# Step 1 of a top-p attention layer: exponentials ahead of the list, a shorter list after tested bounds, two extra tiles in place of three, GpSimd in written order

## The chip, the core and the metric

One NeuronCore of a Trainium2 chip runs the whole program. The metric is the device time of one execution in microseconds; the figure quoted is the median of several executions. VectorE (DVE), ScalarE (ACT), GpSimd (POOL), TensorE (PE; its weight loads are the row PEld) and the SyncE queue (SP) each take their instructions in order.

## The reference

A graph layer makes `x` (3327 rows of 256). A second layer, which is what matters here, then runs two steps of top-p attention and neighbourhood averaging:

```python
q = X @ W1.T @ W2.T;  k = X @ W3.T
probs = softmax(q @ k.T)
sp = probs sorted downwards;  cs = cumsum(sp)
keep = cs - sp < 0.9                    # the fewest columns that hold 0.9 of the row
A = probs * mask(keep);  A = A / max(A.sum(-1), 1e-12)
...
for n in range(2):
    A = top_p_attention(Xa)
    Xf = R @ Xf;  Xa = A @ Xa           # R: sparse adjacency plus identity, rows scaled
    Z = Z + Xf @ U1[n].T + Xa @ U2[n].T
out = layernorm(x + layernorm(x + Z))
```

## The kernel before

The 3327 rows are 26 tiles of 128 rows (the last has 127). Layer 0 and step 0 of layer 1 are untouched by the change. In step 1, item `i` runs from `NT` = 26 to 51, one per tile. The kernel never sorts a whole row. For each tile:

- `some_logits` multiplies q by k into PSUM and ScalarE copies 8 chunks of 416 columns into an array `l` (L1693, L1696).
- `eights` (L1709) takes the eight largest of each group of 167 columns: 20 MAX8, 160 candidates.
- `list_1` and `list_2` sort the first 72 of them, nine rounds of MAX8 and MATCH_REPLACE8 (L1727, L1729). `exp` (L1777) computes the exponentials of the row in two halves with their sums, `exp_list` (L1790) those of the list.
- `list_3` and `settle` make running sums of the list (L1797), find the smallest kept value `t`, the number `d` of ties to drop, and a flag for rows that the list can't settle.
- `mask` drops surplus ties by a MATCH_REPLACE8 over the row (`drop`, L1825) and multiplies by "at least t" (L1811). The result is the tile's attention.
- `product` turns the attention in 7 groups of four 128 x 128 blocks (`turn`: PE transposes, ACT copies) and multiplies it by `xu` (`times`, L1907). Between the groups it runs what `run` has put into seven *slots*. This is the order of the tile loop, for TensorE, ScalarE and VectorE, written out by hand; GpSimd's order in step 1 is the scheduler's.
- `propagate` does the sparse product from 5 gathered blocks (`gather`, L645, issued by GpSimd; `fetch` issues all five at once), `scaled` and `tile_end` add up, normalise twice and store. Mean and variance come from VectorE's batch-norm instructions (`moments`, L1869, L1871).
- `put_aside_1` and `put_aside_2` number the flagged rows and store what is known of each (`pay`: row, maximum, threshold, bound) by an indirect DMA into the table `left_over` (L1981).

Flagged rows are then done as extra ("hard") tiles of 128 rows, `HARD` = 3 of them. `close` at item `NT + CLOSE` (21) ends the first: later rows go to the others. Of an extra tile k, `hard_load` reads the table and gathers the rows, `hard_q` and `hard_exp` make its exponentials, `coarse_bound` tries three bounds on ScalarE with Relu and Sign sums, `bound` tries the rest on VectorE (L1831, one pass over the row each), `hard` takes the values below the bound (L2103), their eights, a list of 72, three `drop`s and the mask (L2132), and `hard_end` multiplies, normalises and stores. `ends` runs the three after the tile loop. If any row stays unsettled or there are too many, a slow version of everything runs after a test at the end.

Of the kernel before, what the change touches and what calls it, by code (L numbers as in the profile page):

```python
# [16 lines left out]
P = 128  # L17
# [73 lines left out]
GROUP = (208, 167)  # L91
LIST = (40, 72)
# [3 lines left out]
HARD = 3  # L96
PAY = 4

COARSE = 3
CUTS = tuple(2.0 ** -f for f in (4.0, 2.0, 1.0, 0.5, 0.25, 0.125))  # L100

CLOSE = 21
# [1069 lines left out]
class Layer1:  # L1172
# [474 lines left out]
    def first_1(self):  # L1647


        while self.phase <= EVERY0 * (NT - 1) + max(AT_0[k] for k in ("sign0", "sign1", "y_out")):  # L1650
            yield
        v = self.item(NT)
        self.item(NT + 1)
        self.fetch(NT)
        v.cand = self.candidates(v.r, GROUP[1], v.tag)
        ready, waiting = [], list(range(-(-N // GROUP[1])))
        for pair in self.chunks():
            while self.done * P < min(NT * P, HALF + pair[0][1] + LC):
                yield
            for i in (NT, NT + 1):  # L1660
                self.some_logits(i, pair)
                yield
            ready += [c for h, s in pair for c in range(h * HALF + s, min(N, h * HALF + s + LC))]
            have = set(ready)
            for g in list(waiting):
                if have.issuperset(range(g * GROUP[1], min(N, (g + 1) * GROUP[1]))):
                    waiting.remove(g)
                    self.eights(v.cand, v.l, v.r, GROUP[1], g * GROUP[1], min(N, (g + 1) * GROUP[1]))
            yield
# [52 lines left out]
    def sort(self, cand, r, length, tag):  # L1722

        nc = self.nc
        lst = self.work.tile([P, length], F32, tag="lst", name=f"lst{tag}")
        for k in range(0, length, 8):
            nc.vector.max(lst[:r, k : k + 8], cand[:r])  # L1727
            if k + 8 < length:
                nc.vector.match_replace(cand[:r], lst[:r, k : k + 8], cand[:r], -BIG)  # L1729
            yield lst  # L1730

    def settle(self, lst, before, last, thr2, r, drop, flag, tag):
# [5 lines left out]
        out = self.work.tile([P, length], F32, tag="outl", name=f"out{tag}")  # L1738
        nc.vector.tensor_scalar(out[:r], before, thr2[:r], None, ALU.is_ge)
        kept = self.work.tile([P, length], F32, tag="kept", name=f"kept{tag}")  # L1740
# [8 lines left out]
        nc.gpsimd.tensor_scalar(lim[:r], last[:r], lst[:r, length - 1 : length], None, ALU.max)  # L1749
        short = self.small("short", f"short{tag}")  # L1750
        nc.gpsimd.tensor_scalar(short[:r], lim[:r], t[:r], None, ALU.is_ge)
        many = self.small("many", f"many{tag}")
        nc.gpsimd.tensor_scalar(many[:r], d[:r], drop + 0.5, None, ALU.is_gt)
        nc.gpsimd.tensor_scalar(flag, many[:r], short[:r], None, ALU.max)
        return t, d, lim

    def list_1(self, i):

        nc, v = self.nc, self.items[i]
        n, r, tag = v.n, v.r, v.tag  # L1760
        if i > NT:
            v.cand = self.candidates(r, GROUP[n], tag)
            self.eights(v.cand, v.l, r, GROUP[n])
        v.last = self.last_eights(v.cand, r, tag)
        v.sort = self.sort(v.cand, r, LIST[n], tag)
        v.lst = next(v.sort)
        v.pay = self.st.tile([P, PAY], F32, tag="pay", name=f"pay{tag}", bufs=3)
        v.nmax, v.thr2 = v.pay[:, 1:2], v.pay[:, 2:3]
        nc.vector.tensor_scalar(v.nmax[:r], v.lst[:r, 0:1], -1.0, None, ALU.mult)
        v.p = self.p[i % 2]  # L1770
        v.sums = self.small("sums", f"sums{tag}", 2)
# [9 lines left out]
    def list_2(self, i):  # L1781
        for _ in self.items[i].sort:
            pass

    def exp_list(self, i):
        nc, v = self.nc, self.items[i]
        r, length = v.r, LIST[v.n]
        v.e = self.work.tile([P, length], F32, tag="e", name=f"e{v.tag}")
        nc.vector.memset(v.e[:, 0:1], 0.0)
        nc.scalar.activation(v.e[:r, 1:], v.lst[:r, : length - 1], AF.Exp, bias=v.nmax[:r])  # L1790

    def list_3(self, i):
# [3 lines left out]
        before = self.work.tile([P, LIST[n]], F32, tag="before", name=f"before{tag}")  # L1796
        nc.vector.tensor_tensor_scan(before[:r], v.e[:r], v.e[:r], 0.0, ALU.add, ALU.add)  # L1797
        nc.vector.tensor_scalar(v.thr2[:r], v.sums[:r, 0:1], v.sums[:r, 1:2], 2.0 * TOP_P, ALU.add, ALU.mult)
# [4 lines left out]
    def mask(self, i):  # L1803
# [5 lines left out]
        self.drop(v.l[:r], v.d, v.t, r, 0, tag)  # L1809
        sA = self.small("sA", f"sA{tag}")  # L1810
        nc.vector.scalar_tensor_tensor(  # L1811
            v.p[:r], v.l[:r, :N], v.t[:r], v.p[:r], ALU.is_ge, ALU.mult, accum_out=sA[:r]
# [21 lines left out]
    def fetch(self, i):  # L1834
# [6 lines left out]
        sh.gather(v.g, table, v.at)  # L1841
        v.m = self.work.tile([P, EB, P], F32, tag="m", name=f"m{v.tag}")
        nc.sync.dma_start(v.m, self.members[v.at])

    def propagate(self, i):
# [6 lines left out]
        nc.tensor.matmul(acc[:r, :D], self.ident[:r, :r], v.y, start=False, stop=True)  # L1852
        v.h1 = self.work.tile([P, D], F32, tag="xf2", name=f"h1_{v.tag}")[:r]
# [11 lines left out]
    def moments(self, src, r, tag):  # L1865
# [8 lines left out]
        return mv  # L1874

# [35 lines left out]
    def scaled(self, i):  # L1911
        nc, v = self.nc, self.items[i]
        v.h = self.work.tile([P, D], F32, tag="xa2", name=f"h{v.tag}")[: v.r]
# [18 lines left out]

    def tile_end(self, i):
# [4 lines left out]
        xb = self.work.tile([P, D], F32, tag="xt", name=f"xb{v.tag}", bufs=3)[:r]  # L1938
        move_rows(nc.sync, xb, sh.xb_rows[on, :], r)
        yield from self.output_rows(h, [xb], r, f"t{v.tag}")  # L1940
# [3 lines left out]
    def put_aside_1(self, i):  # L1944
# [4 lines left out]
        nc.gpsimd.tensor_copy(flag16, flag)  # L1949
        v.pos = self.psm.tile([P, 512], F32, tag="sm", name=f"pos{t}")  # L1950
# [35 lines left out]
    def hard_load(self, k):  # L1986
# [8 lines left out]
        tag_x, width = ("g", EB) if k == 2 else ("hx", 3)  # L1995
        v.x = self.work.tile([P, width, D], F32, tag=tag_x, name=f"x{tag}")
# [11 lines left out]
    def hard_q(self, k):  # L2008
# [14 lines left out]
        v.p = (*self.more, self.p[0])[k]  # L2023
        v.other = (self.l[0][:, :N], self.l[1][:, :N], self.p[1])[k]

        v.top = self.small(f"top{k}", f"top{v.tag}")
        nc.scalar.activation(v.top, v.pay[:, 3:4], AF.Exp, bias=v.pay[:, 1:2])
        nc.gpsimd.tensor_scalar(v.top, v.top, 1.0001, None, ALU.mult)
# [14 lines left out]
    def coarse_bound(self, k, cuts, junk):  # L2043
# [3 lines left out]
        tag = v.tag  # L2047
        less = self.small(f"less{k}", f"less{tag}")
        nc.gpsimd.tensor_scalar(less, v.pay[:, 2:3], 0.5 * (1.0 - 1e-5), None, ALU.mult)
        for f in cuts:  # L2050
            tag = f"{v.tag}_{f}"
            minus = self.small(f"minus{k}", f"minus{tag}")
            nc.gpsimd.tensor_scalar(minus, v.top, -f, None, ALU.mult)
            s = self.small(f"sums{k}", f"sums4{tag}", 4)
            for h in range(2):
                on = slice(h * HALF, min(N, (h + 1) * HALF))
                for j, func in enumerate((AF.Relu, AF.Sign)):
                    nc.scalar.activation(
                        junk[:, on], v.p[:, on], func, bias=minus, accum_out=s[:, 2 * h + j : 2 * h + j + 1]
                    )  # L2060
                    if h == 0 or j == 0:
                        yield
# [13 lines left out]
            yield  # L2076
            yield
            yield

    def bound(self, k, cuts):  # L2080
# [4 lines left out]
        nc.gpsimd.tensor_scalar(v.thr, v.pay[:, 2:3], 0.5, None, ALU.mult)  # L2085
# [11 lines left out]
    def hard(self, k):  # L2097
# [4 lines left out]
        sb = self.small("sb", f"sb{tag}")  # L2102
        nc.vector.scalar_tensor_tensor(other, v.p, top, v.p, ALU.is_lt, ALU.mult, accum_out=sb)  # L2103
        yield
        length = LIST[1]
        cand = self.candidates(P, GROUP[1], tag)
# [3 lines left out]
        for j, lst in enumerate(self.sort(cand, P, length, tag)):  # L2110
            if j == length // 16:
                yield
        e = self.work.tile([P, length], F32, tag="e", name=f"e{tag}")
        nc.vector.scalar_tensor_tensor(e[:, 0:1], thr, 1.0 / TOP_P, sb, ALU.mult, ALU.subtract)
        nc.vector.tensor_copy(e[:, 1:], lst[:, : length - 1])
        before = self.work.tile([P, length], F32, tag="before", name=f"before{tag}")
        nc.vector.tensor_tensor_scan(before, e, e, 0.0, ALU.add, ALU.add)
        flag = self.small("hf", f"hf{tag}")
        t, d, _ = self.settle(lst, before, last, thr2, P, HARD_DROP, flag, tag)

        late = self.small("late", f"late{tag}")
        nc.gpsimd.tensor_scalar(late, before[:, 0:1], thr2, None, ALU.is_ge)
        nc.gpsimd.tensor_scalar(flag, flag, late, None, ALU.max)
        real = self.small("real", f"real{tag}")
        nc.gpsimd.tensor_scalar(real, v.pay[:, 0:1], N - 0.5, None, ALU.is_lt)
        nc.gpsimd.tensor_tensor(self.hflag[:, k : k + 1], real, flag, ALU.mult)
# [11 lines left out]
    def hard_end(self, k):  # L2138
# [13 lines left out]
        v.end = self.output_rows(v.h, [self.b, x1], P, v.tag)  # L2152
# [34 lines left out]
    def ends(self, bounds, older, last):  # L2187


        open_ends, queue = [older, last], []  # L2190

        def more():
            if queue and next(queue[0], True):
                queue.pop(0)
            for g in open_ends[::-1]:
                if next(g, True):
                    open_ends.remove(g)

            for _ in range(2):
                for g in bounds:  # L2200
                    if not next(g, True):
                        break

        def start(k):
            yield from self.hard_q(k)
            for pair in self.chunks():
                yield
                self.hard_exp(k, pair)
            bounds.append(self.coarse_bound(k, CUTS[:COARSE], self.items[f"h{k}"].other))

        def end(k):
            yield from self.hard_end(k)
            open_ends.append(self.items[f"h{k}"].end)

        queue.append(start(2))
        for k in range(HARD):
            if k:
                for _ in bounds[k - 1]:
                    pass
                for _ in self.bound(k, CUTS[COARSE:]):  # L2220
                    more()
            for _ in self.hard(k):
                more()
            queue.append(end(k))
        self.whole()
        while queue or open_ends:
            more()
        for k in range(HARD):
            self.hard_store(k)
# [169 lines left out]
```

## Time and profile before

| | us |
|---|---|
| median of 3 runs (1795.28 to 1797.88) | 1795.72 |
| the profiled execution, its own time | 1795.22 |
| its span, first to last instruction | 1793.4 |
| first product of step 1 begins | 992.2 |
| last product of the tile loop begins | 1588.3 |
| VectorE done with extra tile 0, 1, 2 | 1657.9, 1711.9, 1760.3 |

| engine | busy us | share |
|---|---|---|
| PE | 1483.3 | 83% |
| DVE | 1414.3 | 79% |
| POOL | 1083.7 | 60% |
| ACT | 1023.2 | 57% |

How to read the views: a group or timeline row gives line, engine, operation, output tile <- input tiles, shapes and count; in groups then busy us, mean ns of one, and the idle time before it with what ended it. A row of the waits gives who waited at which line for whom: us in total, times, longest. A row of busy time by stretch gives from:to, its length, then busy us (and instructions) of PE, PEld, DVE, ACT, POOL, the granted PE clock, the DMA share and GB/s. "Idle" of an engine off the path costs nothing.

### The profile page before, as it was taken

The numbers are of one execution on the slowest core, as the hardware profiler recorded it, in microseconds if no ns is written. First come the engines' busy times: TensorE is split into PE (matmuls) and PEld (weight loads), VectorE is DVE, ScalarE is ACT, GpSimd is POOL, SyncE is SP. The second block draws the span as 40 slices with busy tenths as digits, with TensorE's granted clock in tenths as the row PEclk, the third lists the DMA queues.
The fourth block names the chain that finished last, engine by engine and source line by source line (L and its number), as shares of the span: only waits on it lengthen the run. The fifth ranks groups of instructions, "written<-read, shape, count | busy, mean of one in ns | idle before, by whom it ended". The sixth has DMA issues, their size and how long they took to land.

```text
span 1793.4 us, 27513 instructions
## 1 busy us (share of the span) xinstructions
PE 1483.3 (83%) x7995; PEld 998.1 (56%) x7995; DVE 1414.3 (79%) x4757; ACT 1023.2 (57%) x2286; POOL 1083.7 (60%) x1754
## 2 busy tenths in 40 slices
PE   6499999986999999999975999999999989872333
PEld 5256555553555555555543776666766666661333
DVE  5688888438878878878733999999999998787893
ACT  2366666646677777767742555555555555465511
POOL 1477777714666666656643567777777767474311
PEclk8789999987899999999998999999999999895666
DMA  8877774323344434433431222222222212100000
GB/s 237 290 272 236 238 237 123 86 68 96 102 115 122 109 106 116 123 103 105 123 79 51 57 65 69 68 68 68 66 65 66 64 51 77 37 16 21 4 3 3
DMA packets 102440, 179.58 MB, mean 100 GB/s; under 512 B 26401, under 2 KB 64799, under 8 KB 102282
## 3 DMA queue, kind: packets, MB, share of 16 engines
q0 software_dynamic: 26480, 74.24, 16.4%
q1 hardware_dynamic: 57548, 86.65, 14.7%
q10 hardware_dynamic: 18254, 16.86, 3.0%
q8 instruction: 65, 1.06, 0.2%
q14 instruction: 93, 0.76, 0.1%
HBM read 140.58 MB, written 37.21 MB: 99 GB/s over the span
## 4 chain that ended last, share of the span: by engine, by line
DVE 33%; PE 27%; POOL 17%; issue 11%; ACT 6%; DMA 5%; ACTq 1%; POOLq 0%; DVEq 0%
POOL g L645 8%; DVE cand L1709 6%; DVE array L1825 5%; DVE cand L1729 4%; DVE lst L1727 4%; DMA g<-x1k,uidx 3%; PE pl L1693 2%; DVE p L1811 2%; DVE array L1811 2%; POOL g L1525 2%; PE pav L1586 2%; PE pc L1349 2%; PE pavh L1907 2%; PE pav L1907 2%; PE pxf L1329 1%
## 5 line engine op out<-in xcount | busy, mean ns | idle before, releaser
L1907 PE MATMUL pav<-xu,at 128*128 128x256 f32 (+2 forms) x1352 | 331.4, 390 | 6.3 <-ACT at L1893 6.3
L1907 PEld LDWEIGHTS pav<-xu,at 128*128 128x128 f32 (+2 forms) x1352 | 246.1, 191 | 85.9 <-ACT at L1893 39.3
L1709 DVE MAX8 cand<-array 128x8 f32<-128x167 f32 (+5 forms) x921 | 241.5, 336 | 19.2 <-ACT array L1696 18.9
L1696 ACT COPY array<-pl 128x416 f32<-128x416 f32 (+3 forms) x402 | 183.1, 509 | 109.2 <-PE pl L1693 106.8
L1693 PE MATMUL pl<-kT,qT 64*128 64x416 f32 (+3 forms) x804 | 202.6, 566 | 8.4 <-ACT array L1696 4.5
L1893 ACT COPY at<-pt 128x512 f32<-128x512 f32 (+2 forms) x182 | 95.9, 542 | 143.2 <-PE pt L1891 143.0
L645 POOL DMA_INDIRECT g<-whx,edge x130 | 140.3, 1079 | 46.0 <-issue 36.2
L645 POOL DMA_INDIRECT g<-y_rows,edge x130 | 136.1, 1047 | 45.6 <-issue 29.8
L645 POOL DMA_INDIRECT g<-x_rows,edge x130 | 133.4, 1026 | 44.0 <-issue 33.5
L1525 POOL DMA_INDIRECT g<-x1k,uidx x130 | 136.6, 1051 | 32.2 <-issue 29.3
L1727 DVE MAX8 lst<-cand 128x8 f32<-128x160 f32 (+3 forms) x364 | 113.6, 312 | 8.1
L864 DVE FIND_INDEX8 at<-ones,array 128x8 uint32<-128x840 f32 (+1 forms) x104 | 105.5, 1027 | 0.0
L1693 PEld LDWEIGHTS pl<-kT,qT 64*128 64x128 f32 (+1 forms) x804 | 65.7, 187 | 69.0 <-issue 48.7
L1625 POOL TENSOR_TENSOR x<-x,c 128x256 f32<-128x256 f32 (+1 forms) x26 | 28.5, 1095 | 110.2 <-ACT c L1620 110.2
L1825 DVE MATCH_REPLACE8 array<-gone,array 128x3335 f32<-128x3335 f32 (+1 forms) x26 | 94.0, 3617 | 0.0
L1729 DVE MATCH_REPLACE8 cand<-lst,cand 128x160 f32<-128x160 f32 (+3 forms) x312 | 92.9, 298 | 0.0
L1926 POOL TENSOR_TENSOR h<-h,xb 128x256 f32<-128x256 f32 (+1 forms) x26 | 84.1, 3236 | 2.0
L1851 PE MATMUL pxf<-g,m 128*128 128x256 f32 (+1 forms) x260 | 67.5, 410 | 4.0 <-DVE base L1973 4.0
L985 PE MATMUL acc<-g,m 128*128 128x259 f32 (+1 forms) x260 | 65.0, 398 | 6.8 <-ACT m L981 6.8
L1851 PEld LDWEIGHTS pxf<-g,m 128*128 128x128 f32 (+1 forms) x260 | 50.1, 201 | 35.5 <-issue 24.0
L1586 PE MATMUL pav<-g,w 128*128 128x257 f32 (+1 forms) x260 | 62.6, 388 | 3.4 <-DVE w L1580 3.4
L1593 DVE TENSOR_SCALAR rA<-pav 128x1 f32<-128x1 f32 (+1 forms) x26 | 4.1, 158 | 77.1 <-PE pav L1586 77.1
(535 smaller groups left out, 3749.8 us busy)
## 6 DMA issues: line engine op xcount, KB each, us to landing
array<-in_adj_dram SPq DMA_DIRECT2D x23, 1248.0 KB
array<-in_adj_dram SPq DMA_DIRECT2D x23, 415.5 KB
members<-m SPq DMA_DIRECT2D x26, 320.0 KB
m<-members SPq DMA_DIRECT2D x26, 320.0 KB
whx<-table ACTq DMA_DIRECT2D x25, 129.5 KB
x_rows<-x ACTq DMA_DIRECT2D x25, 128.0 KB
x1k<-x ACTq DMA_DIRECT2D x25, 128.0 KB
xb_rows<-xb SPq DMA_DIRECT2D x25, 128.0 KB
```

Of the source, the lines that this page charges most:

```text
L645: self.nc.gpsimd.indirect_dma_start(out=dst[:, b, :], out_offset=None, in_=table[:, :], in_offset=bass.IndirectOffsetOnAxis(ap=self.edge[: ...
L864: nc.vector.max_index(at[:r, g, :], self.ones8[:r], ad[:r, g, :])
L1525: nc.gpsimd.indirect_dma_start(out=v.g2[:, b, :], out_offset=None, in_=sh.x1k[:, :], in_offset=bass.IndirectOffsetOnAxis(ap=v.idx[:, b : b ...
L1586: nc.tensor.matmul(v.acc[:r, : D + 1], v.w[:, b, :r], v.g2[:, b, : D + 1], start=(b == 0), stop=(b == UB - 1))
L1693: nc.tensor.matmul(pl[:r, :w], q[on], self.sh.kT[on, n, s : s + w], start=True, stop=True)
L1696: nc.scalar.copy(l[:r, h * HALF + s : h * HALF + s + w], pl[:r, :w])
L1709: self.nc.vector.max(cand[:r, g * 8 : g * 8 + 8], src[:r, g * group : min(N, (g + 1) * group)])
L1727: nc.vector.max(lst[:r, k : k + 8], cand[:r])
L1729: nc.vector.match_replace(cand[:r], lst[:r, k : k + 8], cand[:r], -BIG)
L1825: nc.vector.match_replace(rev, gone[:r], rev, -BIG)
L1851: nc.tensor.matmul(acc[:r, :D], v.m[:, b, :r], v.g[:, b, :], start=(b == 0), stop=False)
L1907: nc.tensor.matmul(v.acc[: v.r, :D], at[:k, j - 4 * g, : v.r], V[:k, j, :], start=(j == 0), stop=(j == NT - 1))
```

## The change

In each tile of step 1 the exponentials now come first. The groups have 104 columns (32 groups, 256 candidates). `highest` takes the row's maximum from the groups' first ranks, `exp_candidates` the exponentials of the candidates, and `list_1`, now on exponentials, tests four bounds (the maxima over groups of ranks 2 to 5): what the candidates at or above each add up to. Candidates above the best bound that is still short of the threshold are taken as one sum, and only 32 of the rest are sorted. `mask` works on the exponentials in place. Logits are computed three items ahead in place of two. Mean and variance of a tile come from two ScalarE passes with accumulators (`sums`, `by_sums`); extra tile 1 keeps the batch-norm form.

There are two extra tiles. The first closes behind tile 15, is loaded at tile 16, gets its exponentials at tile 17 and three coarse bounds on ScalarE in slots of tiles 18 to 24; its bounds and list on VectorE (`hard_first`) stand beside the last product. The second has two coarse and four fine bounds. GpSimd's order in step 1 is now written order too, and the gathers of the next tile are issued one by one in slots 2 to 6. In `hard`, settling's small operations move from GpSimd to VectorE.

```diff
-GROUP = (208, 167)
-LIST = (40, 72)
+GROUP = (208, 104)
+LIST = (40, 32)
+HARD_LIST = 72
+TRIED = (2, 6)
-HARD = 3
+HARD = 2
-COARSE = 3
+COARSE = (3, 2)
-CLOSE = 21
+CLOSE = 15
...
+    def highest(self, i):
...
+        nc.vector.tensor_reduce(v.nmax[:r], self.ranks(v.cand, r)[:, :, 0], AX.X, ALU.max, negate=True)
...
+    def list_1(self, i):
+        by_rank = ec[:r].rearrange("p (g e) -> p e g", e=8)
...
+        nc.vector.tensor_scalar(v.thr2[:r], v.sums[:r, 0:1], v.sums[:r, 1:2], 2.0 * TOP_P, ALU.add, ALU.mult)
+        nc.vector.tensor_reduce(high[:r], by_rank[:, first:end, :], AX.X, ALU.max)
+        v.last = self.last_eights(ec, r, tag)
+        for j in range(tried):
+            nc.vector.scalar_tensor_tensor(
+                v.cand[:r], ec[:r], high[:r, j : j + 1], ec[:r], ALU.is_ge, ALU.mult, accum_out=above[:r, j : j + 1]
+            )
+        nc.vector.tensor_scalar(over[:r], above[:r], 2.0, v.thr2[:r], ALU.mult, ALU.is_ge)
+        nc.vector.scalar_tensor_tensor(high[:r], over[:r], 2.0, high[:r], ALU.mult, ALU.max)
+        nc.vector.tensor_reduce(skip[:r], high[:r], AX.X, ALU.min)
+        nc.vector.scalar_tensor_tensor(v.cand[:r], ec[:r], skip[:r], ec[:r], ALU.is_lt, ALU.mult)
+        nc.vector.scalar_tensor_tensor(above[:r], over[:r], 0.5, above[:r], ALU.is_lt, ALU.mult)
+        nc.vector.tensor_reduce(v.e[:r, 0:1], above[:r], AX.X, ALU.max)
+        for _ in self.sort(v.cand, r, LIST[1], tag, v.lst):
+            pass
...
     def mask(self, i):
-        self.drop(v.l[:r], v.d, v.t, r, 0, tag)
+        self.drop(v.p[:r], v.d, v.t, r, 0, tag)
-            v.p[:r], v.l[:r, :N], v.t[:r], v.p[:r], ALU.is_ge, ALU.mult, accum_out=sA[:r]
+            v.p[:r], v.p[:r], v.t[:r], v.p[:r], ALU.is_ge, ALU.mult, accum_out=sA[:r]
...
+    def sums(self, h, r, tag):
+        nc.scalar.activation(junk[:r], h, AF.Identity, accum_out=s[:r])
+        nc.gpsimd.tensor_scalar(minus[:r], s[:r], -1.0 / D, None, ALU.mult)
+        yield
+        nc.scalar.activation(junk[:r], h, AF.Square, bias=minus[:r], accum_out=sq[:r])
+        nc.gpsimd.tensor_scalar(mv[:r, 1:2], sq[:r], 1.0 / D, LN_EPS, ALU.mult, ALU.add)
+        nc.gpsimd.tensor_tensor(mv[:r, 1:2], mv[:r, 1:2], self.power[:r], ALU.pow)
+        nc.gpsimd.tensor_tensor(mv[:r, 0:1], minus[:r], mv[:r, 1:2], ALU.mult)
+        yield
+        nc.scalar.activation(h, h, AF.Identity, bias=mv[:r, 0:1], scale=mv[:r, 1:2])
...
     def run(self):
-        with self.tc.manual_schedule(engines=engines):
+        with self.tc.manual_schedule(engines=engines | {mybir.EngineType.Pool}):
...
+                beside = self.propagate(i)
+                slot(1, next, beside)
+                slot(2, next, beside, None)
+                if i + 3 < total:
+                    for k, pair in enumerate(self.chunks()):
+                        slot((0, 1, 2, 6)[k], self.some_logits, i + 3, pair)
                 if i + 1 < total:
                     self.list_1(i + 1)
+                    slot(0, self.list_2, i + 1)
+                if i + 2 < total:
+                    for pair in self.chunks():
+                        slot(1, self.largest, i + 2, pair)
+                    slot(1, self.highest, i + 2)
+                    slot(3, self.exp_candidates, i + 2)
+                    slot(3, self.exp, i + 2, 0)
+                    slot(4, self.exp, i + 2, 1)
...
+                    slot(0 if late else 3, self.put_aside_2, i)
+                    slot(3, self.mask, i + 1)
...
+                for g in (1, 2, 5):
                     slot(g, next, older, None)
                     slot(g, next, last, None)
...
+                    for b, g in enumerate((2, 3, 4, 5, 6)):
+                        slot(g, self.neighbour, i + 1, b)
+                if closing == 1:
                     slot(0, self.hard_load, 0)
...
+                    first = self.hard_first()
+                    for g in range(7):
+                        slot(g, next, first, None)
                     slot(0, self.hard_load, 1)
...
     def ends(self, first, older, last):
+        for pair in self.chunks():
+            self.hard_exp(1, pair)
+            more()
+        for _ in self.coarse_bound(1, CUTS[: COARSE[1]], self.items["h1"].other):
+            more()
+        for _ in first:
+            pass
+        for _ in self.hard_end(0):
+            more()
...
+        for _ in self.bound(1, CUTS[COARSE[1] :]):
+            more()
+        for _ in self.hard(1):
+            more()
+        self.whole()
...
+        for _ in self.hard_end(1):
+            pass
```

## The prediction

> **What bounds the kernel now.** The page gives one profiled execution: 1795.22 us in all, span 1793.4, against a median of 1795.72; I sum against the span and add 1.8 at the end. The edit touches step 1 alone, so I asked first for busy time by stretch.
>
> ```profile
> core 0: us, PE busy (x) PEld busy (x) DVE busy (x) ACT busy (x) POOL busy (x), PEclk, DMA share, GB/s
> 1268.74:1291.86 23.12, 21.62 (x110) 16.13 (x109) 22.10 (x69) 12.72 (x25) 16.80 (x27) 1.00 0.24 66
> 1605.00:1660.00 55.00, 13.49 (x41) 7.03 (x40) 42.51 (x89) 27.58 (x41) 29.25 (x58) 0.54 0.08 22
> 1660.00:1711.00 51.00, 15.53 (x70) 12.77 (x69) 43.36 (x87) 21.89 (x30) 16.35 (x41) 0.67 0.01 3
> 1711.00:1761.00 50.00, 16.06 (x79) 13.85 (x79) 47.52 (x102) 5.63 (x11) 8.19 (x18) 0.67 0.01 3
> ```
>
> The first row is one ordinary tile: 23.12 us, VectorE 22.10 of it, TensorE 21.62. The other rows are the extra tiles: VectorE fills them and TensorE is a third busy. The chain of waits says the same: up to 1476 it is VectorE's mask (L1825, L1811) and eights (L1709), tile after tile; from 1628 it is VectorE three times over, each time with L1709, three L1825 and L2132 in turn. The timeline of the third extra tile shows what one costs:
>
> ```profile
> 1712.20 3.68 DVE L1831 SCALAR_TENSOR_TENSOR p<-array,cndh 128x3327 f32<-128x3327 f32 x1
> 1716.56 3.69 DVE L1831 SCALAR_TENSOR_TENSOR p<-array,cndh 128x3327 f32<-128x3327 f32 x1
> ...
> 1729.95 4.73 DVE L1709 MAX8 candh<-p 128x8 f32<-128x167 f32 x20
> ...
> 1760.13 0.16 DVE L2135 RECIPROCAL rAh<-rAh 128x1 f32<-128x1 f32 x1
> ```
>
> A tested bound takes 4.36 us (1712.20 to 1716.56), the tile 48.4 (1711.9 to 1760.3). Behind it stand 33.1 us of product, norms and store, to 1793.4. Between 1477 and 1588 the waits have VectorE idle too:
>
> ```profile
> DVE before L1797 <- ACT e L1790: 14.6, 3, 6.0
> DVE cand L1709 <- ACT array L1696: 5.9, 2, 3.5
> ```
>
> So the last ordinary mask, due near 1569 at 23.1 a tile, ends at 1588.3. Landmarks: the first product begins at 992.2, the last at 1588.3, extra tiles are done on VectorE at 1657.9, 1711.9 and 1760.3.
>
> **What the Trainium skill says.** "SBUF — State Buffer", section on its two sides: a VectorE op with two SBUF inputs and a GpSimd op exclude each other for a whole instruction. The trace agrees:
>
> ```profile
> 1356.62 3.85 DVE L1811 SCALAR_TENSOR_TENSOR array<-array,t,array 128x3327 f32<-128x3327 f32 x1
> ...
> 1357.07 3.99 POOL L1926 TENSOR_TENSOR h<-h,xb 128x256 f32<-128x256 f32 x1
> ```
>
> The add takes 0.73 alone, and ends after the mask. In return L1815, one element, takes 0.56 us here and 0.16 where GpSimd is quiet. The change brings VectorE seven more such ops a tile. "ScalarE: Activation LUTs", section on table sets: a set switch costs 2.7 us; the page doesn't list all of the set with exp. This trace has Square, Exp, Identity, Relu and Sign with a single table load (at 9.0 us), so the new Square costs no switch.
>
> **VectorE per ordinary tile.** Prices come from the groups by form:
>
> ```profile
> L1709 DVE MAX8 cand<-array 128x8 f32<-128x208 f32 x360 | 105.9, 361 | 0.0
> L1727 DVE MAX8 lst<-cand 128x8 f32<-128x160 f32 x225 | 73.6, 327 | 6.1
> L1729 DVE MATCH_REPLACE8 cand<-lst,cand 128x160 f32<-128x160 f32 x200 | 61.7, 309 | 0.0
> L1034 DVE SCALAR_TENSOR_TENSOR n<-rz,n 128x256 f32<-128x256 f32 x25 | 10.6, 423 | 1.8 <-ACT n L1032 1.6
> ```
>
> Between 167 elements (318 ns) and 208 (361) an element is 1.05 ns. Removed: 20 eights of 167, 4.69 (0.234 apart); nine rounds on 160 candidates, 6.51 with the maximum (0.78 each); two pairs of batch norm, 1.08; list settling on 72, 1.64. Together 13.9.
> Added: 32 eights of 104, each 0.234 less 63 x 1.05 ns = 0.168, so 5.4, and their maximum 0.3. Four tested bounds on 256 candidates: L1034's 0.42 with a read of the accumulator is 0.49 apart, 2.0. A last masked copy on 256, 0.35. Six small steps around them (threshold, bounds, skip), 1.2. Four rounds on 256: MAX8 0.327 + 0.10, replace 0.309 + 0.10, so 0.99 a round and 3.4 in all. Settling on 32: 1.2. Together 13.8. Mask, drop and the index stay at 9.2. The sum is 23.0 against 23.1: **nothing is gained in the loop itself.** The shorter list pays for the tests, and the lost batch norms for more groups. Against GpSimd each of the seven two-input ops may lose up to 0.4 (L1815's difference): 0 to 2.8, and I take 0.3, since L1034 holds 405 to 469 ns amid busy GpSimd gathers. Below nothing: independent small ops can overlap more than I count, to 22.2 or so. Period: 23.3.
>
> **What lies beside it.** TensorE's work per tile is unchanged, 21.6. ScalarE gets four passes over 256 elements for mean and square (0.49 as L1914, 0.6 with the accumulator: 2.4) and the exponentials of 256 candidates (0.5), loses 0.35: 12.7 becomes 15.3 of 23.3. exp of tile i+2 sits in slot 3 and waits for a maximum that VectorE has at about 14 us into the tile; queued behind it are the copy of turn 6 and the second exp, and TensorE wants that copy at about 17: just covered. GpSimd, now in written order, stands at settling's first op until VectorE has the cut, 8.4 us in; then 15.9 us of ops (five gathers 6.5, put-aside store 1.1, four adds 2.9, moments 2.7, flags 2.6) and up to 3.4 shut out by the mask: it ends 27.7 in. It next has to stand ready at 23.3 + 8.4 = 31.7: four us of cover. The last gather lands 2.8 after issue, 28.3, TensorE uses it near 30.6.
>
> **Start of the loop.** Before, exp ran beside the sort. Now, after the last eights (977.3, two tiles' worth), maximum and exponentials of candidates 0.9, both halves of exp 3.75, bounds and list 7.1, settling 1.5, drop and mask 8: the first product begins at 998.5, 6.3 later.
>
> **The first extra tile moves into the loop.** It closes behind tile 15 and loads at tile 16: its load has GpSimd wait for a DMA (2.3 in the trace) and issue two gathers (2.6), 4.9 against four of cover; on SP its load stands behind the next tile's y and members, whose issues take 0.32 and 0.38; TensorE adds 5.0 for its q and logits where it has 1.7 spare. ScalarE's coarse trials, three bounds of 6.7 us, spread over seven tiles at 3.7 each beside 15.3: covered. I put these at 4 us (0 to 12), in place of some 19 lost before.
>
> **The sum.** 24 periods 559.2; tile 25's cut and mask without eights 17.3; so the last product begins at 998.5 + 559.2 + 17.3 + 4 = 1579. Extra tile 0 on VectorE then: three bounds 13.2, the below sum 3.8, eights 5.5, nine rounds on 256 8.8, settling and flags 3.2 (eight small ops come over from GpSimd), three drops 12.4, mask 4.1: 51, so 1630 (before 69.6 from the same point). Extra tile 1: one bound more, 55.4, so 1685.5; its own exps and two coarse bounds end near 1621 beside it. A third tile, 48.4, is gone. Then 33.1 as before: 1718.6, with 1.8 about **1720.5, and 0.5 for the median: 1721**, 75 less. By part: start +6, loop -15, extra tiles -66.
>
> **Rivals.**
> - *TensorE sets the loop.* If VectorE comes to 21.9 or less, 24 tiles give 34 us more: 1687. For it: 21.62 busy of 23.12. Against: my count stays above 22.
> - *The shared port costs more.* 1.3 us a tile beyond my 0.3: 1752. For it: L1815 and L1926. Still faster.
> - *GpSimd's order becomes the bound.* Its 27.7 us stand; the cover is only that the next tile wants it late. If any of its last ops (gather, add) holds TensorE or ScalarE at the tile's start, the period is 27.7: 1721 + 24 x 4.4 = 1827, **slower**. It decides from a period of 26.4 on (75/24 more). Against: the places counted above.
> - *Two extra tiles don't hold the rows.* Then the slow path runs after all of this, and the time is far above; nothing here prices it. Four bounds before a list of 32 may flag more rows than 72 sorted ones did; no view shows how many.
>
> **Chances.** Forecast 0.72, TensorE 0.12, port 0.09, GpSimd 0.05, slow path 0.02. The range takes in the first three, 1686 to 1760. About 0.2% is what a measurement here can tell from no change: faster 0.93, same 0.01, slower 0.06.
>
> **What would show it.** Tile period 23.3 with VectorE above 95% busy; eights 0.17 apart; last product from 1579; VectorE of extra tile 0 under the last product, done near 1630, and 33 us from VectorE's last mask to the end. Wrong if the period is off by one us, if GpSimd's gathers head the waits of TensorE, or if bounds of extra tile 1 wait for ScalarE.

## The result, and the profile after

The changed kernel takes **1815.21 us** (median of 5 runs, 1812.24 to 1823.96) against 1795.72 (5 runs, 1794.91 to 1803.66) for the kernel before beside it: a ratio of 1.0107, interval 1.0073 to 1.0141. It is 1% slower. The forecast was 1721, 4% faster. The profiled execution took 1817.99 us, its span is 1816.2. Beside the first four experiments below (e1 to e4) the kernel before took 1869.84 us, and their first mask was done at 1060 to 1070, 61 to 71 us later than here, for a reason that no run shows; of these four only the ratio and the loop are compared.

Laid beside the forecast, the loss stands in three places and nowhere else ("mask" is VectorE's last operation of a tile's mask, L1853, behind which the tile's product begins):

| | forecast | measured | difference |
|---|---|---|---|
| first product begins (first mask done) | 998.5 | 999.0 | +0.5 |
| last product begins (26th mask done) | 1579 | 1650.3 | +71 |
| VectorE waits ahead of extra tile 0's bounds | 0 | 7.7 | +7.7 |
| extra tile 0 on VectorE | 51 | 51.2 | 0 |
| VectorE waits within extra tile 1's bounds | 0 | 19.4 | +19.4 |
| extra tile 1 on VectorE | 55.4 | 54.7 | -0.7 |
| from there to the end | 33.1 | 32.6 | -0.5 |

The tile loop takes 651.3 us from the first mask to the 26th, that is 26.05 for each of its 25 intervals, where the forecast's 580.5 make 23.2. Busy time by stretch (columns as before: from:to, length, then PE, PEld, DVE, ACT, POOL busy, clock, DMA share, GB/s) shows an early tile, a later one, and the three stretches of the end:

```profile
1044.52:1067.56 23.04, 20.22 (x102) 14.68 (x99) 22.02 (x75) 12.21 (x31) 14.86 (x23) 1.00 0.18 49
1331.88:1360.58 28.70, 26.49 (x134) 19.91 (x134) 21.83 (x76) 18.74 (x44) 19.11 (x34) 1.00 0.20 59
1658.10:1709.30 51.20, 28.01 (x108) 18.45 (x107) 49.38 (x109) 15.21 (x41) 37.38 (x43) 0.72 0.14 32
1709.30:1728.90 19.60, 3.33 (x12) 2.66 (x12) 0.17 (x3) 15.84 (x21) 4.36 (x20) 0.50 0.03 7
1728.90:1783.60 54.70, 13.86 (x69) 11.72 (x67) 52.82 (x112) 6.67 (x17) 11.73 (x13) 0.62 0.01 3
```

The first three periods are 22.5, 23.1 and 23.0, as the forecast has them for a full VectorE. From the fourth on they lie between 23 and 33 (the last, of a tile without eights behind it, takes 21.4), and VectorE's work has not grown: 22.02 us in the early tile, 21.83 in the later one, with seven us of idle beside it. So VectorE is no longer what sets the loop. The groups of the page tell who waits (after the bar: busy us, mean ns; then idle us before it, and its releaser):

```profile
L1891 PE MATMUL pxf<-g,m 128*128 128x256 f32 (+1 forms) x260 | 74.6, 413 | 61.6 <-DMA g<-y_rows,edge 61.6
...
L1924 POOL TENSOR_SCALAR minbt<-sbt 128x1 f32<-128x1 f32 (+1 forms) x26 | 27.7, 1065 | 95.6 <-ACT junkbt L1922 95.6
...
L1806 DVE TENSOR_SCALAR pay<-sums 128x1 f32<-128x1 f32 (+1 forms) x26 | 5.5, 210 | 69.1 <-ACT array L1789 38.5
```

The kernel before had no such wait in its sparse product, with the same 260 instructions:

```profile
L1851 PE MATMUL pxf<-g,m 128*128 128x256 f32 (+1 forms) x260 | 67.5, 410 | 4.0 <-DVE base L1973 4.0
```

Three waits, then. TensorE's sparse product waits for the gathers; GpSimd's first step of a norm (`minus` of `sums`, L1924) waits for ScalarE's sum; VectorE's first step of the list (L1806) waits for ScalarE's exponentials. The chain of waits through one slow tile joins them into a ring, a path that comes back to where it began (start, us, what; short pieces and GpSimd's many between 1331 and 1344 left out):

```profile
1318.79 3.94 DMA g<-y_rows,edge
...
1322.77 1.22 PE pxf L1891 x2
1323.99 0.85 PE pxf L1892 x2
1324.84 1.74 PE pl L1691 x4
1326.58 0.89 ACT array L1694 x2
1327.48 0.41 ACT junkbt L1922 x2
...
1327.97 0.37 POOL minbt L1924
1328.34 3.28 issue
...
1344.28 1.30 issue
1345.57 3.80 DMA g<-y_rows,edge
```

Read downwards: the last gather of a tile is issued at 1318.79 and lands 3.94 later. TensorE has stood at the sparse product in slot 1 for it. Only then come the logits of slot 1, their copies on ScalarE, and in ScalarE's order behind these the sum of the tile before. GpSimd has been waiting for that sum:

```profile
1321.61 0.29 POOL L1756 TENSOR_SCALAR flag<-many,short 128x1 f32<-128x1 f32 x1
1327.97 3.68 POOL L1924 TENSOR_SCALAR minbt<-sbt 128x1 f32<-128x1 f32 x1 [6.07 <-ACT junkbt L1922]
1331.62 0.20 POOL L1924 TENSOR_SCALAR minat<-sat 128x1 f32<-128x1 f32 x1
```

It waits 6.07 us, and its one-element operation then stands beside VectorE's mask (L1848, 1327.88 to 1331.57) for 3.68, where the next one takes 0.20. That is the exclusion which the Trainium skill states ("SBUF — State Buffer", section on two separate sides), of a VectorE operation with two SBUF inputs and a GpSimd operation that reads SBUF. Only behind it come the moments and then, spread among the put-aside steps and the norm's multiply and add, the next five gathers; the last is issued at 1345.57, 26.8 us after the one at the top. Each engine in the ring waits for the one ahead of it. VectorE, which hangs on it through ScalarE's exponentials, comes last:

```profile
1337.90 0.21 DVE L1806 TENSOR_SCALAR pay<-sums 128x1 f32<-128x1 f32 x1 [5.85 <-ACT array L1789]
```

At the end, VectorE's own waits (waiter <- releaser: us in total, times, longest) give the other 27 us:

```profile
DVE cndh L2159 <- POOL toph_0.25_19533 L2147: 19.4, 1, 19.4
...
DVE idx L2050 <- POOL far L2025: 7.7, 1, 7.7
```

The first is extra tile 1: its first fine bound waits for the second coarse one, which ends on ScalarE at 1726.8. The second is the last tile's put-aside index: GpSimd comes to it (L2025, at 1657.8) only behind the last moments, a gather and the small operations of a coarse bound.

### The profile page after: what moved, and what is told of

It reads as the page before. It is cut to its first block, busy times and chain, and to the rows that moved or that the text cites. A ratio compares the mean times of both kernels' runs of the same rounds, so it can differ in the third digit from the quotient of the medians.

```text
span 1816.2 us, 27633 instructions
## 1 busy us (share of the span) xinstructions
PE 1487.6 (82%) x7891; PEld 983.5 (54%) x7891; DVE 1376.0 (76%) x4881; ACT 1044.9 (58%) x2462; POOL 1074.8 (59%) x1747
## 4 chain that ended last, share of the span: by engine, by line
PE 32%; POOL 20%; DVE 16%; issue 14%; DMA 9%; ACT 8%; ACTq 1%; POOLq 0%; DVEq 0%
POOL g L647 9%; PE pav L1966 5%; PE pl L1691 4%; DMA g<-y_rows,edge 4%; DMA g<-x1k,uidx 3%; PE pav L1588 2%; PE pc L1351 2%; POOL g L1527 2%; DVE cand L1812 2%; PE pxf L1331 2%; DVE e L1726 1%; DVE cand L1728 1%; PE plt L1563 1%; PE pxf L1891 1%; PE pt L1950 1%
## 5 line engine op out<-in xcount | busy, mean ns | idle before, releaser
L1966 PE MATMUL pav<-xu,at 128*128 128x256 f32 (+2 forms) x1352 | 349.0, 404 | 32.9 <-ACT at L1952 32.9
L1966 PEld LDWEIGHTS pav<-xu,at 128*128 128x128 f32 (+2 forms) x1352 | 254.5, 199 | 116.3 <-ACT at L1952 52.9
L1707 DVE MAX8 cand<-array 128x8 f32<-128x104 f32 (+5 forms) x1233 | 260.3, 286 | 10.9 <-ACT array L1694 10.4
L1691 PE MATMUL pl<-kT,qT 64*128 64x416 f32 (+3 forms) x804 | 211.1, 588 | 9.8 <-ACT array L1694 8.7
L647 POOL DMA_INDIRECT g<-y_rows,edge x130 | 150.2, 1156 | 49.0 <-issue 39.4
L1891 PE MATMUL pxf<-g,m 128*128 128x256 f32 (+1 forms) x260 | 74.6, 413 | 61.6 <-DMA g<-y_rows,edge 61.6
L1627 POOL TENSOR_TENSOR x<-x,c 128x256 f32<-128x256 f32 (+1 forms) x26 | 28.3, 1088 | 118.9 <-ACT c L1622 118.9
L1924 POOL TENSOR_SCALAR minbt<-sbt 128x1 f32<-128x1 f32 (+1 forms) x26 | 27.7, 1065 | 95.6 <-ACT junkbt L1922 95.6
L1896 POOL TENSOR_TENSOR h<-h,x 128x256 f32<-128x256 f32 (+1 forms) x26 | 32.3, 1244 | 43.1 <-ACT h L1895 43.1
L1806 DVE TENSOR_SCALAR pay<-sums 128x1 f32<-128x1 f32 (+1 forms) x26 | 5.5, 210 | 69.1 <-ACT array L1789 38.5
L1950 PE MATMUL pt<-ident,array 128*128 128x128 f32 x338 | 51.7, 280 | 6.7 <-DVE array L1848 6.7
```

The source lines that it names most:

```text
L647: self.nc.gpsimd.indirect_dma_start(out=dst[:, b, :], out_offset=None, in_=table[:, :], in_offset=bass.IndirectOffsetOnAxis(ap=self.edge[: ...
L1691: nc.tensor.matmul(pl[:r, :w], q[on], self.sh.kT[on, n, s : s + w], start=True, stop=True)
L1707: self.nc.vector.max(cand[:r, g * 8 : g * 8 + 8], src[:r, g * group : min(N, (g + 1) * group)])
L1891: nc.tensor.matmul(acc[:r, :D], v.m[:, b, :r], v.g[:, b, :], start=(b == 0), stop=False)
L1950: nc.tensor.transpose(pt[: rows(j), j - j0, :r], v.p[:r, cols(j)], self.ident[:r, :r])
L1966: nc.tensor.matmul(v.acc[: v.r, :D], at[:k, j - 4 * g, : v.r], V[:k, j, :], start=(j == 0), stop=(j == NT - 1))
```

## The experiments

**Theory A**: the ring above sets the loop: written GpSimd order, gathers at the end of it, and a sparse product in slot 1 that needs them. **Theory B**: GpSimd simply has too much work per tile. **Theory C**: ScalarE, with exponentials, sums and coarse bounds, is too full. **Theory A2** for the end: the coarse bounds of extra tile 1 on ScalarE come too late for VectorE.

Of each run I give the median, the ratio to the kernel before beside it, and the loop: first mask to 26th mask in the profiled execution. Two executions of the changed kernel differ by 5 us in the loop, so differences of that size say nothing.

| kernel | loop us | a tile | median us | ratio to before (interval) |
|---|---|---|---|---|
| changed kernel | 651.3 | 26.05 | 1815.21 | 1.0107 (1.0073-1.0141) |
| changed kernel again (a0) | 646.1 | 25.8 | 1808.62 | 1.0091 (1.0059-1.0123) |
| e1 all gathers in slot 0 | 607.0 | 24.3 | 1828.65 | 0.9806 (0.9758-0.9854) |
| e2 sparse product in slots 4, 5 | 594.2 | 23.8 | 1818.13 | 0.9731 (0.9698-0.9764) |
| e3 batch norm | 634.0 | 25.4 | 1862.69 | 0.9959 (0.9940-0.9978) |
| e4 GpSimd's order free | 719.1 | 28.8 | 1939.97 | 1.0370 (1.0335-1.0404) |
| e5 no coarse bounds for tile 1 | 647.3 | 25.9 | 1798.85 | 1.0024 (1.0009-1.0039) |
| e6 = e2 and e5 | 595.1 | 23.8 | 1745.99 | 0.9740 (0.9696-0.9783) |
| e7 = e6, four coarse for tile 0 | 595.0 | 23.8 | 1753.36 | 0.9783 (0.9743-0.9824) |
| e8 = e2, one coarse for tile 1 | 594.4 | 23.8 | 1744.70 | 0.9729 (0.9713-0.9745) |
| e9 sums in slots 3, 4, 6 | 676.1 | 27.0 | 1839.26 | 1.0250 (1.0228-1.0271) |
| e10 gathers a slot earlier | 626.9 | 25.1 | 1790.03 | 0.9981 (0.9953-1.0008) |
| e11 = e6, less GpSimd work | 582.9 | 23.3 | 1735.30 | 0.9678 (0.9661-0.9695) |

**a0: the changed kernel beside the later runs.** 

> The changed kernel unchanged, as the baseline on the chip of the experiments. All theories: before step 1 it needs what the other kernels need on this chip; first product to last mask 651 us (26.05 a tile), last mask to end 166. If this chip takes about 61 us longer ahead of step 1, as the first experiments did, about 1876, ratio to before 1.00 to 1.01.

1808.62 us, loop 646.1, first mask done at 995: e5 to e11 can be compared in microseconds too. The trace also bears on the mask's part in the ring. In the first trace the mask shuts L1924 out in seven tiles (2.9 to 3.7 us each), and periods of 28 to 30 alternate with such of 23 to 26; here it does so in three. Yet periods 4 to 15, ahead of the first extra tile, average 26.4 against 26.5: by these two traces the lock-out of this one operation makes the periods uneven, not long.

**e1: the gathers ahead of the ring.** The edit:

```diff
-                    for b, g in enumerate((2, 3, 4, 5, 6)):
+                    for b, g in enumerate((0, 0, 0, 0, 0)):
```

> All five gathers of the next tile issued in slot 0, ahead of GpSimd's wait for the first ScalarE sum, instead of one each in slots 2 to 6. Theory A (a loop: last gathers behind GpSimd's wait for ScalarE's sum, that sum behind logits copies, those behind the sparse product on TensorE, that behind the landing of the gathers): the loop is cut, the tile period falls from 26.2 us to VectorE's 23.2, and 24 x 3.0 = 72 us go: about 1743. Theory B (GpSimd simply has more than 26 us of work and lock-outs a tile, in any order): period stays near 26, 1805 to 1820. Theory C (ScalarE is too full and exp is late by itself): also stays, 1800 or more, with VectorE still waiting for exp's sums.

The loop falls from about 650 to 607.0, with GpSimd's instructions the same. Periods 4 to 15 average 23.4, about VectorE's own length, with the sparse product still in slot 1, so slot 1 is not too early by itself. What is left stands in the later periods (16 to 19 average 27.5, 20 to 24 25.6), where the first extra tile is loaded and tried, and where VectorE still waits 23 us for exponentials. TensorE's list of waits (1090 to 1640) no longer has the gathers at all; it is headed by the copies of the turned attention:

```profile
PE pav L1966 <- ACT at L1952: 46.5, 29, 4.3
PE so_far L2041 <- POOL flagged L2032: 2.9, 1, 2.9
```

Theory B would have left the loop as it was.

**e2: the sparse product late.** The edit, alone:

```diff
-                slot(1, next, beside)
-                slot(2, next, beside, None)
+                slot(4, next, beside)
+                slot(5, next, beside, None)
```

> The sparse product moved from slots 1 and 2 to slots 4 and 5; the gathers stay where they are. Theory A: the gathers are wanted some 9 us later and no longer stand ahead of the logits copies and sums, so the loop has slack: period 23.2 to 23.5, about 1743 to 1750. Theory B: GpSimd's work is the same, 1805 to 1820. Theory C: 1800 or more.

594.2, the largest single step, and again with all of GpSimd's and ScalarE's work in place. In the stretch from 1090 to 1640 VectorE of the changed kernel waits 64 us for exponentials:

```profile
DVE pay L1806 <- ACT array L1789: 33.6, 7, 6.2
DVE pay L1806 <- ACT p L1789: 30.6, 10, 7.8
```

In the same stretch of this kernel the whole list is

```profile
DVE base L2043 <- PE so_far L2041: 2.3, 1, 2.3
DVE pay L1806 <- ACT p L1789: 0.3, 1, 0.3
```

So VectorE sets the loop again. A stands; B, and C for the loop, fall.

**e3: the norms back on VectorE's batch norm.**

```diff
-        yield from self.by_sums(h, [v.xb], r, f"t{v.tag}")
+        yield from self.output_rows(h, [v.xb], r, f"t{v.tag}")
```

> Tiles take mean and variance from VectorE's batch-norm instructions again, as the kernel before, in place of the two ScalarE sums. Theory A: GpSimd waits for VectorE instead of ScalarE's sum behind the sparse product, so the loop is longer only by VectorE's 1.1 us a tile: period about 24.4, 24 x 1.8 = 43 less, about 1772. Theory B: GpSimd loses only some 0.8 us of work, period 25.5 or more, 1795 to 1815. Theory C: ScalarE is 2.4 us lighter, period 24 to 24.5, about 1770, but then VectorE's wait for exp's sums goes and GpSimd's wait is not what changes.

634.0, 12 to 17 us better, far from e2. At 25.4 a tile it is a miss for A (24.4) and for C (24 to 24.5) and stands near B's 25.5; alone it would decide nothing. It takes the sums off ScalarE, and GpSimd now waits for VectorE instead:

```profile
POOL mvat L1913 <- DVE idx L2050: 84.8, 21, 5.4
```

and the sparse product still waits 34.7 us for gathers. A lighter ScalarE does not bring the loop back, and e2 comes back with all of ScalarE's work.

**e4: GpSimd's order left to the scheduler in step 1, as before.**

```diff
-        with self.tc.manual_schedule(engines=engines | {mybir.EngineType.Pool}):
+        with self.tc.manual_schedule(engines=engines):
```

> GpSimd's order in step 1 left to the scheduler as in the kernel before, all else as changed. Theory A: the scheduler issues the gathers when their buffer is free, ahead of the waits: period 23.2 to 24, 1743 to 1765. Theory B: 1800 or more, since the amount of work is the same. Theory C: 1800 or more.

A miss for A as I had put it, with the written order itself as part of the harm: without it the loop is 719.1. The longest of ScalarE's own waits is now one for GpSimd:

```profile
ACT junkbt L1927 <- POOL minbt L1924: 127.5, 20, 8.0
```

In the chain of one tile the scheduler has five gathers and the put-aside store in front of L1924, and ScalarE's square pass, with the next copies for TensorE behind it, waits for L1924. So leaving the order to the scheduler is no cure: GpSimd's work is the same, and in this chain the gathers stand ahead of the step that ScalarE waits for.

**e5: no coarse bounds of extra tile 1.**

```diff
-COARSE = (3, 2)
+COARSE = (3, 0)
```

> The changed kernel with no bounds of extra tile 1 on ScalarE (all six on VectorE, which has 2 x 4.36 us more to do). Theory A2 (the 19.4 us that VectorE waits for the second bound are the lateness of ScalarE's coarse bounds, which start only after that tile's exponentials): the wait goes, 8.7 us of work come back, so about 10 us less than the changed kernel. Rival (it is the exponentials themselves that are late, for which store, load and gathers on GpSimd are held up): the wait stays at 10 us or more and the time is the same or longer. Loop unchanged at 26.

1798.85 against 1808.62 for a0: 9.8 less, as A2 has it. The wait at L2159 is gone from VectorE's list, the loop is unchanged at 647.3.

**e6: e2 and e5 together.** 

> Sparse product in slots 4 and 5 and no coarse bounds of extra tile 1. Theory A with A2: loop 23.8 a tile as with the late sparse product alone, VectorE without a wait in it; the wait of 12.6 us at the second bound of extra tile 1 goes and 8.7 of work come: 4 us less than the late sparse product alone, ratio to before about 0.97. Rival (exponentials late): no gain or 5 us worse.

1745.99 us: 52.9 less than e5, from the sparse product's place alone, and 2.6% faster than the kernel before. The 4 us expected against e2 are too small for the ratios to show (0.9740 and 0.9731); in the traces the time from the last mask to the end falls from 157.6 to 154.0. By stretch: one tile, the loop, extra tile 0, extra tile 1:

```profile
1113.60:1137.60 24.00, 23.13 (x110) 17.42 (x111) 22.84 (x79) 14.32 (x32) 16.36 (x28) 0.93 0.22 59
995.90:1591.00 595.10, 549.38 (x2685) 412.03 (x2684) 568.51 (x1843) 374.84 (x821) 422.18 (x694) 0.97 0.21 62
1596.00:1648.70 52.70, 24.18 (x103) 16.70 (x102) 50.88 (x111) 14.66 (x40) 35.65 (x44) 0.72 0.15 35
1648.70:1712.50 63.80, 16.57 (x79) 13.93 (x77) 61.64 (x124) 8.95 (x22) 20.35 (x16) 0.63 0.01 4
```

VectorE is busy 568.5 of 595.1 (96%), and for the rest stands in the short gaps between dependent small operations.

**e7: one coarse bound more for extra tile 0.** `COARSE = (4, 0)` on top of e6. 

> As e6, and a fourth coarse bound of extra tile 0 on ScalarE in the loop (20 steps of coarse bounds where tiles 18 to 25 have 24 places), so one bound less on VectorE beside the last product: 4.4 us less than e6 if ScalarE still has room (theory A; it is busy 15 of 23.8 us a tile). Theory C (ScalarE is what fills up): the loop gets longer by 2 us or more over the last tiles, and nothing is gained.

7 us slower than e6, for neither reason given. The loop is 595.0, so ScalarE had the room. But the third bound's last pass ends at 1580.9 and the fourth runs only from 1596.1 to 1603.5, behind the last mask (1591.0), and VectorE waits for it, at the same line as the changed kernel for a bound of extra tile 1:

```profile
DVE cndh L2159 <- POOL 0.7071067811865476_19224 L2147: 13.7, 1, 13.7
```

I had counted places in the slots, not when the last of them comes.

**e8: one coarse bound for extra tile 1.** `COARSE = (3, 1)` with e2's edit. 

> Sparse product in slots 4 and 5, and one coarse bound of extra tile 1 on ScalarE in place of none (e6) or two. In e6 that tile's exponentials end at 1640.7 and VectorE comes free at 1648.7; a coarse bound took 9 to 10 us from the last exponential, so it ends near 1650.5. Theory A2: VectorE waits 2 us and has 4.4 us less to do, 2.5 us less than e6. Rival (what ScalarE and GpSimd do there for the last tiles' norms pushes it further out): no gain, or some us more than e6.

1744.70 with a wait of 2.9 at L2159; 1.3 less than e6, which is less than the runs can tell apart. By medians it stands level with e6; from the last mask to the end the trace has 151.8 against 154.0.

**e9: the ring opened at its other end.**

```diff
-                for g in (1, 2, 5):
+                for g in (3, 4, 6):
                     slot(g, next, older, None)
```

> The changed kernel with one edit: the steps of the two normalisations (sum, square, multiply and add) in slots 3, 4 and 6 in place of 1, 2 and 5. Gathers stay in slots 2 to 6 and the sparse product in slots 1 and 2. Theory A (a ring: last gathers, sparse product, logits, ScalarE's sum in slot 1, GpSimd's wait for it ahead of the next gathers): the ring is opened at its other end, GpSimd gets to the gathers without that wait, and the period falls towards VectorE's, 23.8 to 24.5 a tile, 595 to 612 from first to last mask in place of 646. Rival (a sparse product in slot 1 is too early by itself, whatever GpSimd waits for): TensorE still waits for the gathers, period 25.5 or more.

A miss: 676.1, slower than the changed kernel. The gathers' wait is gone from TensorE, as A has it, but another ring has closed. GpSimd's first wait is now

```profile
POOL h L1896 <- ACT h L1895: 128.2, 19, 10.7
```

In the timeline of one tile GpSimd stands 6.96 us at the add behind the sparse product, is then shut out by the mask (3.92 us), and has two gathers, the put-aside store and the moments behind that; ScalarE waits for the moments at the end of the tile (L1933), with the copy behind it on which TensorE's next product waits 4.14 us. Behind that product comes the next sparse product, and behind this ScalarE's scaling, for which GpSimd stands at the add again: 27.4 us from one add to the next, and 27.4 is the period of most tiles. Neither rule of mine, "period towards 24" nor "TensorE still waits for gathers", holds: opening one ring is not enough where GpSimd's order has another early wait.

**e10: each gather one slot earlier**, (1, 2, 3, 4, 5). 

> The changed kernel with one edit: the five gathers one slot earlier each, (1, 2, 3, 4, 5) in place of (2, 3, 4, 5, 6). Theory A: a dose between the changed kernel (26) and all gathers in slot 0 (24.3): the last gather is off the end of GpSimd's order, the wait of the sparse product for the gathers falls from some 100 us in all to under half, period about 25. Theory B (GpSimd has too much to do a tile): no change, 26, since its work is the same.

626.9, 25.1 a tile, and TensorE's wait for the gathers falls from

```profile
PE pxf L1891 <- DMA g<-y_rows,edge: 42.9, 30, 2.5
```

in the changed kernel's loop to

```profile
PE pxf L1891 <- DMA g<-y_rows,edge: 30.1, 16, 2.8
```

A dose between: what counts is how late the gathers stand in the order. The wait of its weight loads fell from 55.2 to 36.6, so the wait fell by a third and not by half.

**e11: e6 with less GpSimd work.** The edit, on top of e6, leaves out the multiplication by the norm's weights and the add of `x` and bias, so that what the kernel stores is no longer the layer's output; it is here for its time alone:

```diff
         yield from self.sums(h, r, f"a{tag}")
-        nc.gpsimd.tensor_tensor(h, h, self.g[:r], ALU.mult)
-        for term in terms:
-            nc.gpsimd.tensor_tensor(h, h, term, ALU.add)
         yield
```

> e6 with work left out on GpSimd: the multiplication by the first norm's weights and the add of x and bias between the two norms (two operations of 0.73 us a tile). VectorE has the same instructions. Question: why does VectorE need 23.8 to 24.0 us a tile in e6 where the forecast had 23.3 and the changed kernel's first three tiles 22.5 to 23.1. Rival of the forecast (the shared port): with fewer GpSimd operations to shut its two-input operations out, the period falls by up to 0.7 to 23.1-23.3. If the operations are long for another reason: 23.8 as in e6.

The loop falls from 595.1 to 582.9, 0.5 a tile, with VectorE's instructions the same: their busy time in it falls from 568.5 us to 553.5 (in the changed kernel it was 551.0). The group of one two-input operation (L1822, on 256 elements) shows where, first in e6:

```profile
L1822 DVE SCALAR_TENSOR_TENSOR cand<-ec,skip 128x256 f32<-128x256 f32 x23 | 18.1, 785 | 0.8
```

and in e11:

```profile
L1822 DVE SCALAR_TENSOR_TENSOR cand<-ec,skip 128x256 f32<-128x256 f32 x24 | 12.4, 516 | 0.9
```

In e6 L1822 takes 0.73 to 1.04 us in the 18 tiles where a GpSimd multiply or add of 256 elements runs beside it, mostly the two that e11 leaves out, and 0.48 to 0.49 in the other eight. So the forecast's rival "the shared port costs more" is real and small. Not all of it is undone: the tests (L1812) take 600 ns in e6 and 590 in e11, against 490 in the changed kernel.

## Why the prediction was wrong, step by step

- **Right: VectorE per tile, start, extra tiles, tail.** 23.0 us forecast for VectorE's work, and 23.0 to 23.1 measured in the second and third period. The parts hold too, so the sum is not luck: in the second period the eights took 5.43 us (5.4 forecast), the four tests 2.11 (2.0), the four rounds 3.40 (3.4). In e1 periods 4 to 15 come to 23.4, in e11 the whole loop to 23.3 a tile. Also right: first product 999.0 for 998.5; the two extra tiles 51.2 and 54.7 for 51 and 55.4; tail 32.6 for 33.1.
- **Wrong: GpSimd's "four us of cover".** The step that failed is "It next has to stand ready at 23.3 + 8.4 = 31.7". It asked for one appointment of GpSimd only, settling's first operation. There was an earlier one: L1924 in slot 1 needs a sum that ScalarE has behind the logits, which TensorE has behind the sparse product, which needs GpSimd's own last gathers. From L1924 to the last gather's issue GpSimd needs 17.6 us in the traced tile (the mask's 3.3 included), from there to the next sum 9.2: 26.8, and no cover in it, since each piece waits for the one before. In "the last gather lands 2.8 after issue, 28.3, TensorE uses it near 30.6" the landing was short too: 3.8 and 3.9 in this ring, though the median of the loop is 3.0.
- **The third rival named it, at 5%.** "If any of its last ops (gather, add) holds TensorE or ScalarE at the tile's start" is what happened, with a period of 26.05 in place of 27.7. That the two lie close is chance: 27.7 starts at settling and counts its 8.4 us of waiting, which is no part of the ring. 26.05 is below the 26.4 from which it was to decide; the loop's 71 us nearly ate the 75 of the gain, and the end's 27 did the rest. e2 shows what this one place is worth: with the sparse product moved, 26.05 is 23.8, which is 57 of the loop's 71 us, and e6 from end to end is 1745.99, inside the range of 1686 to 1760. All three signs by which the forecast was to be known wrong were there: the period, the gathers at the head of TensorE's waits, and the bounds of extra tile 1 waiting for ScalarE.
- **Wrong: "two coarse bounds end near 1621 beside it".** In the changed kernel they end at 1726.8, or 76 us after the last product begins where the forecast had 42, and VectorE had been done with extra tile 0 since 1709.3. The store, load and gathers of tile 1 stand in GpSimd's order between the last tiles' norms, and some of them were held up beside VectorE's bounds (the put-aside store, 1.03 us in the tile above, took 5.66). A2, e5: without these bounds 9.8 us less.
- **Too small: the shared port.** 0.3 us a tile taken, "0 to 2.8" given; e11 gives 0.5 for two of GpSimd's operations, and e6's 23.8 against the forecast's 23.2 is of that size.
- **Too small: the wait ahead of extra tile 0.** 7.7 us, for the last tile's put-aside index on GpSimd, was in no step. It stays at 5.0 in e6.
- **Within its range: extra tile 0 in the loop.** "4 us (0 to 12)" was taken. The four periods from its closing to its first trials (16 to 19) take 116.0 us in the changed kernel, 10 more than four at the 26.5 ahead of them, which is part of the 71. There VectorE waits 9.2 us for the count of flagged rows in `close` (L2043), a step that was not priced. In e6 that wait is 0.9 and the four periods take 99.2, some 3.4 more than four of the ordinary 23.9.

What stays open: how much of the ring is the mask shutting GpSimd out (3.3 us of 26.8 in the traced tile). By a0 it does not hang on L1924, but there the mask held the add behind it (L1896) more often, and no run moved the mask alone.

## What to carry to other kernels

When an engine's order is written by hand, follow each of its waits to what releases it, and on to what that releaser waits for: if the path comes back to a later instruction of the same engine, it is a ring, and its length, not the engine's busy time, is the period (26.8 us in the tile traced here, 27.4 in e9, with GpSimd busy for 15 to 20 in most periods). Issue transfers ahead of an engine's first wait (e1), or use them late in the tile (e2): moving one user from slot 1 to slot 4 was worth 53 us here. A list of free places for background work says nothing on its last one; ask when it ends and who waits for that.

## What the runs showed of the hardware

A one-element GpSimd operation took 3.68 us beside a two-input VectorE pass over 3327 elements and 0.20 just after. Issuing an indirect transfer on GpSimd suffers in the same way: in e6, from 990 us on, the 19 that began inside a two-input VectorE pass over 3327 elements took 3.3 to 5.8 us, and the other 140, those beside MATCH_REPLACE8 over the row included, 1.0 to 1.3. The other way round, a two-input VectorE operation on 256 elements took 0.73 to 1.04 us beside a GpSimd add or multiply of that size, and 0.48 to 0.49 without one (e6, L1822). An indirect gather landed 2.8 to 7.2 us after issue in the changed kernel's loop, median 3.0.
